# Two fused layers in fp32: one row sum in fp32, a first period in another order, and a scale and shift put off by way of memory

## The chip, the cores and the metric

The kernel runs on one core of a Trainium2 chip. A core has TensorE (PE, matmuls; PEld is its weight load), VectorE (DVE), ScalarE (ACT), GpSimd (POOL) and SyncE (SP), which mainly issues DMAs. The engines have separate in-order instruction streams and meet through semaphores. The metric is the device time of one execution in microseconds (us), as the median of several; smaller is better. The profile is of one execution, with time counted from its first instruction.

## What is computed

Four images of 64 by 64 positions with 256 channels pass through two layers, all in float32.

```python
# layer A: attention over the 4096 positions of an image
f, g, v = xt @ Wf + bf, xt @ Wg + bg, xt @ Wh + bh          # 32, 32, 128 channels
beta = softmax(einsum('bqd,bkd->bqk', g, f), axis=-1)
x = x + (einsum('bqk,bkd->bqd', beta, v) @ Wo + bo).reshape(b, h, w, c)
# layer B: triangle attention, 8 heads of 32, then a feed-forward
scores = einsum('bilhd,bljhd->biljh', q, k) / sqrt(d_k)
att = softmax(scores, axis=2)
out = einsum('biljh,bilhd,bljhd->bijhd', att, v1, v2)
h = layer_norm(x_in + out.reshape(B, N, N, E) @ Wo, ln_agg_g, ln_agg_b)
mlp = relu(h @ W1 + b1) @ W2 + b2
return layer_norm(mlp + h, ln_out_g, ln_out_b)               # scale ln_out_g, shift ln_out_b
```

## The kernel before

`run` goes through the images b = 0 to 3 in turn: layer A by `layer0`, then layer B by `first_layer1` (b = 0) or `next_layer1` (b = 1 to 3). The feed-forward of an image (class `Tokens`, instance `rest`) is not done in its own layer B but is woven into the layer B of the next image, 16 tiles of 256 positions; that of the last image ends in `alone`. So the feed-forward of image 0 runs in the layer B of image 1, that of image 1 in the layer B of image 2, and those of image 2 and of part of image 3 in the layer B of image 3. The schedule is by hand (`tc.manual_schedule`): each engine runs its instructions in the order in which the program issues them, and only the semaphores are put in by the framework.

**Layer A.** `layer0` walks 64 groups g, eight for each of eight blocks of 512 queries (`qb, k = divmod(g, 8)`). `score` makes four 128x512 score tiles in fp32r (L544), ScalarE takes their exponentials e (L556), and `values` multiplies them with v in fp32 (L571), while VectorE adds e up in esum (L578). At k = 7 the row sums of the block are made: VectorE folds esum to 512 columns (L581), writes a rounded fp32r part (L583), the sum once more in fp32 (L584), and the rest of it, sum minus part, again as fp32r (L585). `norm` multiplies both parts with a matrix of ones (L592), which adds them over the partitions in one PSUM tile den; the reciprocal (L594) and a product with o (L596) follow. The list `parts` spreads the projections of the block before over the groups k, each with its stores on SP. After the last block its parts stand apart: `norm(last)`, for an older image's feed-forward two `heads`, a projection, `output(last)` (y, L617), and then, mixed, the first scores of layer B, the rest of the projections and the first feed-forward tile. GpSimd has no work within the groups of layer A for b > 0.

**Layer B.** 32 steps (4 head pairs times 8 groups of rows), two of them in a period. A step has eight products of 128x2048 elements: att times v2 (`product`, L989), to be multiplied on TensorE with a sparse matrix of v1 (`accumulate`, L999) into the PSUM tiles acc. For b > 0 GpSimd makes three of the eight in even steps and two in odd ones (`npool`: the last ones, m = 5, 6, 7 or 6, 7), from a copy of att in SBUF; VectorE makes the others, with att in PSUM. VectorE's buffers R are three, GpSimd's buffers Rp two; a buffer is free when TensorE has accumulated it. ScalarE copies a finished acc out (`take`, L1009).

The order is the list `ORDER`: each word is a piece of work, and `/n` says by how many periods late it works (word `A05/1` in period p is the accumulation of product 5 of step 2(p-1)). Words: R product, A accumulate, T take, S sums, W weights, V the sparse matrix, t and c the turned attention weights; sp and e0, e1 a tile of scores and its exponentials for later periods, sf, f0, f1 the same for the first one alone; h0, h1 the heads of a feed-forward tile (L1058, L1063), sa its statistics, fa its first normalisation, ht, hT, hU the turned copies, m0, m1 and r0, r1 the hidden layer, z0, z1 its output (L1211), so the output's statistics (L1089, L1093), rr and pp the roots and their polishing (on GpSimd, L1119 to L1130), fo the last normalisation, and fi the last scale and shift. fi calls `finish`: two operations of 128x512 on GpSimd (L1225, L1226) and a store on SP (L1227). The tile z that it works on has tag s4, which has two buffers; the turned copies hT2 of the feed-forward use the same tag.

In steps 24 to 32 of a layer B the next image's inputs of layer A are fetched (`ahead.fetch` on SP, `ahead.spread` by DMAs that GpSimd issues, L260 and L266), for b < 3.

Of the kernel before, what the change touches and what calls it, by code (L numbers as in the profile page):

```python
# [10 lines left out]
F32 = mybir.dt.float32  # L11
# [4 lines left out]
ALU = mybir.AluOpType  # L16
AX = mybir.AxisListType

P = 128
C = 256  # L20
# [9 lines left out]
NP = T // 256  # L30
# [12 lines left out]
ORDER = """  # L43
    r0/1 A10/2 A11/2 m1/1 R14/2 R05/1 S1/1 R15/2 T10/2 sp/1 A14/2 A16/2 r1/1 e0/1 e1/1 A15/2 A05/1 T11/2 R04/1
    A04/1 z0/1 W1/1 R03/1 V1/1 fi/2 S0 z1/1 t1/1 so/1 R06/1 R00/1 c1/1 sa A03/1 R07/1 R02/1 A06/1 A02/1 A00/1
    rr/1 pp/1 W0 R01/1 A07/1 A01/1 fo/1 fa T01/1 R12/1 t0 T00/1 sf/1 R17/1 h1/-1 R13/1 f0/1 h0/-1 ht f1/1 R16/1
    hU A13/1 hT A12/1 A17/1 R11/1 c0 R10/1 m0 V0
""".split()

# [17 lines left out]
def attention_then_triangle_kernel(  # L67
# [422 lines left out]
    def layer0(b, F, safe, rest, ahead):  # L490
# [70 lines left out]
        def values(g, ahead):  # L561
            qb, k = divmod(g, 8)
            tt, n = divmod(k, 4)
            if k == 0:
                o_ps[qb] = pc("o")
                esum[qb] = work.tile([P, 4, QB], F32, tag="Rp", name="esum")
            es = e.pop(g)
            for r in range(4):
                if ahead:
                    score(g + 1, r)  # L570
                nc.tensor.matmul(  # L571
                    o_ps[qb], F.v[tt][:, r * 4 + n, :], es[:, r, :],
                    start=(k == 0 and r == 0), stop=(k == 7 and r == 3),
                )
            if k == 0:
                nc.vector.tensor_copy(esum[qb], es)
            else:
                nc.vector.tensor_tensor(esum[qb], esum[qb], es, ALU.add)  # L578
            if k == 7:
                halves = esum[qb]  # L580
                nc.vector.tensor_tensor(halves[:, 0:2], halves[:, 0:2], halves[:, 2:4], ALU.add)  # L581
                part = parts_of[qb] = work.tile([P, 2, QB], PART, tag="hid", name="part", bufs=1)
                nc.vector.tensor_tensor(part[:, 0], halves[:, 0], halves[:, 1], ALU.add)  # L583
                nc.vector.tensor_tensor(halves[:, 2], halves[:, 0], halves[:, 1], ALU.add)  # L584
                nc.vector.tensor_tensor(part[:, 1], halves[:, 2], part[:, 0].bitcast(F32), ALU.subtract)  # L585


        def norm(qb):
            den, part = pb("den") if qb < last else pa("den")[:, 0, :], esum.pop(qb)[:, 2, :]
            two = parts_of.pop(qb)  # L590
            for h in range(2):
                nc.tensor.matmul(den, ones_f, two[:, h], start=(h == 0), stop=(h == 1))  # L592
            rec = work.tile([P, QB], F32, tag="es", name="rec0")
            nc.vector.reciprocal(rec, den)  # L594
            oT[qb] = work.tile([P, QB], F32, tag="hT", name="oT")
            nc.vector.tensor_tensor(oT[qb], o_ps.pop(qb), rec, ALU.mult)  # L596
            ends[qb] = ((den, ALU.min), (part, ALU.max))
# [125 lines left out]
        for g in range(8 * NQB):  # L723
            qb, k = divmod(g, 8)
            if b == 0 and not safe:
                for load in later[3 * g : 3 * g + 3]:
                    load()
                if g == 6:
                    fold_bias()
                if g == 20:  # L730
                    add_b2()
            if safe and k == 0 and qb + 1 < NQB:
                mx, todo = pieces(qb + 1)
                for qc, t in todo:
                    max_piece(qc, t, mx)
                row[qb + 1] = max_row(mx)
            values(g, g + 1 < 8 * NQB)

            if qb > 0 and not (qb == last and k >= 6 + late):
                for part in parts[k]:  # L740
                    part(qb - 1)
            if late and g % 2 == 0 and 0 <= g // 2 - 2 < ahead.n:
                ahead.bring(g // 2 - 2)
            if late and g % 2 == 1 and 0 <= g // 2 - 3 < ahead.n:
                ahead.turn(g // 2 - 3)
            if qb == last and k == 3:
                L.fetch_v1(0)
                L.fetch_v1(1)
            if qb == last and k == 5:
                if b > 0:  # L750
                    rest.load(NP * (b - 1))
                L.fetch_qk(0, True)
# [273 lines left out]
    class Tokens:  # L1026
        def __init__(self):
            self.ios = []
            self.A, self.htp = {}, {}
            self.h, self.hT, self.hT2, self.hid, self.z, self.zp, self.hps = {}, {}, {}, {}, {}, {}, {}  # L1030
            self.mv = self.rs = None

        def load(self, tt, far=False):
            b, t = divmod(tt, NP)
# [394 lines left out]
    def next_layer1(b, L, rest, ahead, F):  # L1429
# [32 lines left out]
        def of_piece(word, q):  # L1462
# [9 lines left out]
            elif word == "sa" and first:  # L1472
                moments(q - 1)
                rest.stats(rest.hps[t0 + q], 0)
            elif word == "so" and second:
                moments(q)
                z = rest.z[t0 + q] = work.tile([P, 2, C], F32, tag="s4", name="z")
                rest.sums_of(rest.zp[t0 + q], z, rest.mv, 2)
            elif word == "rr" and second:
                moments(q)  # L1480
                rest.roots(0 if q + 1 < n1 else 2, 4)
                rs[q] = rest.rs
            elif word == "pp" and second:
                moments(q)
                rest.rs = rs.pop(q)
                rest.polish(0 if q + 1 < n1 else 2, 4, nc.gpsimd, back=back_t)
                rn[q] = rest.rn
            elif word == "fa" and first:
                rest.rn = rn[q - 1]
                rest.affine_a(tt)  # L1490
            elif word == "fo" and second:
                rest.rn = rn[q]
                rest.affine_o(tt)
            elif word == "ht" and first:
                rest.turn(tt)
            elif word == "hT" and first:
                rest.normed(tt)
            elif word == "hU" and first:
                rest.carried(tt)
            elif word in ("m0", "m1") and first:  # L1500
                n = int(word[1])
                mps[q][n] = [rest.hidden(tt, fc) for fc in (2 * n, 2 * n + 1)]
            elif word in ("r0", "r1") and first:
                n = int(word[1])
                for fc, mp in zip((2 * n, 2 * n + 1), mps[q][n]):
                    rest.rectify(tt, fc, mp)
            elif word in ("z0", "z1") and second:
                n = int(word[1])
                rest.outputs(tt, n, new=tt not in rest.zp)
                mps.setdefault(q, {})["z", n] = True  # L1510
            elif word == "fi" and second:
                rest.finish(tt)

        def spread(step):
            if F is not None:
# [4 lines left out]
        for period in range(NP + 4):  # L1520
            for word, late in words_of(ORDER):
                i = period - late
                if word[0] in "RATSWVtc":
                    step_word(word[0], 2 * i + int(word[1]), int(word[-1]))
                elif word in ("sp", "sf"):
                    if (i == 0) == (word == "sf"):
# [77 lines left out]
```

## Time and profile before

| what | value |
|---|---|
| runs shown | 3672.42 us median of 3 (3669.09 to 3676.33) |
| the profiled execution | 3669.47 us, its span 3667.7 us |
| TensorE busy | 3543.8 us (97%) |
| VectorE busy | 2725.4 us (74%) |
| ScalarE busy | 1935.7 us (53%) |
| GpSimd busy | 1760.0 us (48%) |
| L989 on GpSimd | 328 products, 4574 ns each |
| L989 on VectorE | 696 products, 2274 ns each |
| L1225 and L1226 on GpSimd | 48 each, 1288 and 1289 ns |
| L578 on VectorE | 224 adds, 2289 ns each |
| the chain that ended last | PE 67%, POOL 10%, issue 5%, DVE 4%, ACT 2% |

A busy time is the sum over an engine's instructions; since the engines work side by side, a share says little of what bounds a stage. The chain of waits is followed back from the last instruction to whatever released it. "idle before" names the engine whose work ended a wait. An fp32 matmul shows as two records, an fp32r matmul as one.

### The profile page before, as it was taken

To read this page: it belongs to the slowest core of one execution; us is meant where nothing else is said; L and a number is where in the kernel's file an instruction comes from. 1 tells how busy PE (TensorE), PEld (TensorE's weight loads), DVE (VectorE), ACT (ScalarE), POOL (GpSimd) and SP (SyncE) were. 2 spreads that over 40 slices of the span, in tenths; PEclk is the share of its full clock that TensorE was granted. 3 is DMA by queue.
4 is the path that set the end of the run, shared out by engine and by line. 5 is a ranking of instruction groups with operands and counts; after the bars stand their busy time and mean duration, and the time that the engine had idled before them with its cause. 6 is when DMAs were issued, how large, how long until landed. Compare 5 with 4: busy or idle time off the path is not lost.

```text
span 3667.7 us, 58399 instructions
## 1 busy us (share of the span) xinstructions
PE 3543.8 (97%) x22410; PEld 1909.1 (52%) x22410; DVE 2725.4 (74%) x2334; ACT 1935.7 (53%) x4209; POOL 1760.0 (48%) x918
## 2 busy tenths in 40 slices
PE   9999899889999999998999999999899999999998
PEld 6555444434555555553455555554455555555477
DVE  4777599997555489999555549999755556999976
ACT  3444455544444466765444446776444436777654
POOL 5000199994000089999000029999600005999920
PEclk9999999999999999999999999999999999999999
DMA  9544565464111444325311154333511125441221
GB/s 174 139 134 119 135 156 140 113 148 112 57 53 52 107 101 98 91 55 93 77 49 55 49 140 93 86 82 62 117 43 52 49 82 132 96 93 49 68 68 53
DMA packets 478769, 336.59 MB, mean 92 GB/s; under 512 B 301648, under 2 KB 432464, under 8 KB 469648
## 3 DMA queue, kind: packets, MB, share of 16 engines
q1 hardware_dynamic: 429440, 305.80, 31.5%
q0 software_dynamic: 36160, 19.94, 5.1%
q10 hardware_dynamic: 12880, 7.01, 0.7%
q8 instruction: 179, 2.93, 0.3%
q14 instruction: 110, 0.90, 0.1%
HBM read 188.95 MB, written 143.65 MB: 91 GB/s over the span
## 4 chain that ended last, share of the span: by engine, by line
PE 67%; POOL 10%; issue 5%; DVE 4%; ACT 2%; DMA 0%; ACTq 0%; POOLq 0%; DVEq 0%
PE o L571 18%; PE acc L999 16%; POOL Rp L989 8%; PE proj L632 6%; PE zp L1211 5%; PE mp L1191 5%; PE s L544 5%; PE hp L1058 3%; PE sp L887 2%; DVE R L989 2%; PE v1p L664 2%; PE y L617 1%; PE att L941 1%; PE hp L1063 1%; PE htp L1158 1%
## 5 line engine op out<-in xcount | busy, mean ns | idle before, releaser
L989 POOL TENSOR_TENSOR Rp<-attP,v 128x2048 f32<-128x2048 f32 x328 | 1490.6, 4574 | 403.6 <-ACT attP L949 368.9
L989 DVE TENSOR_TENSOR R<-att,v 128x2048 f32<-128x2048 f32 x696 | 1548.4, 2274 | 81.3 <-PE acc L999 62.9
L571 PE MATMUL o<-e,v 128*128 128x512 f32 x2048 | 1043.6, 592 | 0.0
L578 DVE TENSOR_TENSOR esum<-esum,e 128x2048 f32<-128x2048 f32 x224 | 512.7, 2289 | 518.0 <-ACT e L556 515.1
L556 ACT ACTIVATE e<-s 128x1024 f32<-128x1024 f32 x512 | 523.3, 1023 | 580.8 <-PE s L544 482.0
L544 PE MATMUL s<-gT,fT 128*128 128x512 f32 x1024 | 785.3, 769 | 8.1 <-ACT e L556 5.1
L999 PE MATMUL acc<-R,wsel 128*32 128x512 f32 x5568 | 704.4, 601 | 31.2 <-DVE R L989 20.0
L1119 POOL TENSOR_SCALAR nt<-mv 128x4 f32<-128x4 f32 (+1 forms) x51 | 9.8, 192 | 1204.1 <-DVE mv L1075 1200.0
L571 PEld LDWEIGHTS o<-e,v 128*128 128x128 f32 x2048 | 388.6, 190 | 275.9 <-issue 233.7
L999 PE MATMUL acc<-Rp,wsel 128*32 128x512 f32 x2624 | 345.4, 598 | 32.9 <-POOL Rp L989 32.3
L1009 ACT COPY ao<-acc 128x1024 f32<-128x1024 f32 x256 | 254.3, 1021 | 183.5 <-PE acc L999 146.4
L999 PEld LDWEIGHTS acc<-R,wsel 128*32 128x32 f32 x5568 | 152.6, 109 | 377.4 <-issue 279.7
L544 PEld LDWEIGHTS s<-gT,fT 128*128 128x128 f32 x1024 | 194.0, 190 | 243.5 <-issue 230.5
L924 ACT ACTIVATE es<-S,rd 128x64 f32<-128x64 f32 x1024 | 257.9, 336 | 16.7 <-DVE rd L916 13.9
L1191 PE MATMUL mp<-hT,w 128*128 128x256 f32 x1024 | 249.5, 389 | 0.7 <-ACT hT L1163 0.7
L1211 PE MATMUL zp<-w,hid 128*128 128x256 f32 x1024 | 245.0, 385 | 0.8 <-ACT hid L1200 0.8
L1191 PEld LDWEIGHTS mp<-hT,w 128*128 128x128 f32 x1024 | 186.7, 190 | 101.3 <-ACT attP L949 36.0
L1211 PEld LDWEIGHTS zp<-w,hid 128*128 128x128 f32 x1024 | 185.6, 190 | 62.4 <-issue 31.9
L594 DVE RECIPROCAL rec<-den 128x512 f32<-128x512 f32 x32 | 107.4, 3357 | 125.2 <-PE den L592 125.2
L999 PEld LDWEIGHTS acc<-Rp,wsel 128*32 128x32 f32 x2624 | 80.7, 110 | 220.1 <-issue 124.9
L1200 ACT ACTIVATE hid<-mp,b_sb 128x256 f32<-128x256 f32 x256 | 105.3, 470 | 117.7 <-PE mp L1191 117.7
L897 ACT ACTIVATE S<-sp 128x512 f32<-128x512 f32 x128 | 129.8, 1116 | 64.5 <-PE sp L887 64.5
(177 smaller groups left out, 3563.0 us busy)
## 6 DMA issues: line engine op xcount, KB each, us to landing
v<-v2d SPq DMA_DIRECT2D x44, 512.0 KB
v1c<-v1d SPq DMA_DIRECT2D x128, 128.0 KB
aT<-ao SPq DMA_DIRECT2D x1024, 16.0 KB
A<-aT SPq DMA_DIRECT2D x256, 64.0 KB
out_dram<-z SPq DMA_DIRECT2D x63, 256.0 KB
y<-yT SPq DMA_DIRECT2D x56, 256.0 KB
q<-st SPq DMA_DIRECT2D x56, 256.0 KB
k<-st SPq DMA_DIRECT2D x52, 256.0 KB
```

The lines of the kernel that those rows point to most:

```text
L544: nc.tensor.matmul(s_ps[r // 2][:, r % 2, :], fT[tt][:, ts(r * 4 + n, P)], gT[qb // 4][:, ts(qb % 4, QB)], start=True, stop=not safe,)
L556: nc.scalar.activation(e[g][:, 2 * j : 2 * j + 2, :], s_ps[j], AF.Exp)
L571: nc.tensor.matmul(o_ps[qb], F.v[tt][:, r * 4 + n, :], es[:, r, :], start=(k == 0 and r == 0), stop=(k == 7 and r == 3),)
L578: nc.vector.tensor_tensor(esum[qb], esum[qb], es, ALU.add)
L632: nc.tensor.matmul(ps, w[:, cc, rows], y(qb, cc), start=(cc == 0), stop=(cc == 1))
L897: nc.scalar.activation(self.S[pair][:, :, l0 : l0 + 8].rearrange("p i l -> p l i"), sp[:, lh], AF.Copy if self.safe else AF.Exp,)
L924: nc.scalar.mul(e[:, i, :], rows[:, i, :], rec[:, i : i + 1])
L989: eng.tensor_tensor(R, src.unsqueeze(1).to_broadcast([P, D, N]), v2[h], ALU.mult)
L999: nc.tensor.matmul(acc[32 * c : 32 * c + 32, n % 2, :], w[:, n, c, 16 * h : 16 * h + 32], R[:, ts(c, 8), :].rearrange("p d j -> p (d j)"), ...
L1009: nc.scalar.copy(self.ao[step][:, ts(np, 2)].rearrange("p k d j -> p k (d j)"), self.acc[step][np])
L1191: nc.tensor.matmul(self.mp[:, fc % 2, :], w1_sb[:, cc, ts(fc, P)], self.hT[tt][:, cc, :], start=(cc == 0), stop=(cc == 1),)
L1211: nc.tensor.matmul(zp[:, n, :], self.hid[tt][:, fc, ts(n, P)], w2_sb[:, fc, :], start=(fc == 0), stop=(fc == 3 and tt not in self.hT2),)
```

## The change

It has three parts.

1. For the last block of layer A (`qb == last`) VectorE no longer writes the two fp32r parts: after the fold it makes one fp32 sum, and `norm` multiplies it with the ones in one fp32 matmul.
2. In `ORDER`, h1 stands ahead of sf, and h0 ahead of f0. sf, f0 and f1 do something in the first period only, so only there does the order change. For step 0 the accumulations of products 5 and 4 change places.
3. For b = 1 and 2, fi calls `put_off` in place of `finish`: the normalised tile is stored unscaled to DRAM. In the layer A of the next image, `recall` loads a tile back at every third group, and `finish` scales, shifts and stores it two groups later. The layer B of image 3 keeps `finish`.

```diff
 ORDER = """
-    rr/1 pp/1 W0 R01/1 A07/1 A01/1 fo/1 fa T01/1 R12/1 t0 T00/1 sf/1 R17/1 h1/-1 R13/1 f0/1 h0/-1 ht f1/1 R16/1
+    rr/1 pp/1 W0 R01/1 A07/1 A01/1 fo/1 fa T01/1 R12/1 t0 T00/1 R17/1 h1/-1 sf/1 R13/1 h0/-1 f0/1 ht f1/1 R16/1
...
             if k == 7:
                 halves = esum[qb]
                 nc.vector.tensor_tensor(halves[:, 0:2], halves[:, 0:2], halves[:, 2:4], ALU.add)
+                if qb == last:
+                    nc.vector.tensor_tensor(halves[:, 2], halves[:, 0], halves[:, 1], ALU.add)
+                    return
...
         def norm(qb):
             den, part = pb("den") if qb < last else pa("den")[:, 0, :], esum.pop(qb)[:, 2, :]
-            two = parts_of.pop(qb)
-            for h in range(2):
-                nc.tensor.matmul(den, ones_f, two[:, h], start=(h == 0), stop=(h == 1))
+            if qb < last:
+                two = parts_of.pop(qb)
+                for h in range(2):
+                    nc.tensor.matmul(den, ones_f, two[:, h], start=(h == 0), stop=(h == 1))
+            else:
+                nc.tensor.matmul(den, ones_f.bitcast(F32), part, start=True, stop=True)
...
+            if b > 1 and g % 3 == 0 and g < 3 * NP:
+                rest.recall(NP * (b - 2) + g // 3)
+            if b > 1 and g % 3 == 2 and g < 3 * NP:
+                rest.finish(NP * (b - 2) + g // 3)
...
+            self.raw = {}
+        def put_off(self, tt):
+            b, t = divmod(tt, NP)
+            if t == 0:
+                self.raw[b] = dram.tile([NP, P, 2, C], F32, tag="raw", name="raw")
+            nc.sync.dma_start(out=self.raw[b][t], in_=self.z.pop(tt))
+
+        def recall(self, tt):
+            b, t = divmod(tt, NP)
+            self.z[tt] = work.tile([P, 2, C], F32, tag="s4", name="z")
+            nc.sync.dma_start(out=self.z[tt], in_=self.raw[b][t])
...
             elif word == "fi" and second:
-                rest.finish(tt)
+                (rest.finish if own else rest.put_off)(tt)
...
-                if word[0] in "RATSWVtc":
+                if i == 0 and word in ("A05", "A04"):
+                    for m in (4, 5) if word == "A04" else ():
+                        step_word("A", 0, m)
+                elif word[0] in "RATSWVtc":
                     step_word(word[0], 2 * i + int(word[1]), int(word[-1]))
```

## The prediction

> **What bounds the kernel now.** I read the page's slices first, then windows by stage, the waits of each engine in a stage, and the timeline where a stage starts or ends. Times are us from the span's start; A and B name the two layers (spatial attention, triangle attention).
>
> ```profile
> PE   9999899889999999998999999999899999999998
> POOL 5000199994000089999000029999600005999920
> ```
>
> Each digit is a fortieth of the span. TensorE is full nearly everywhere. GpSimd is empty in each image's layer A and full in layer B, where it takes 5 of every 16 products (L989) and the scale and shift L1225, L1226. Windows over images 1, 2, 3 (bounds; length; then busy PE, PEld, DVE, ACT, POOL; clock; DMA):
>
> ```profile
> 1760.00:2130.00 370.00, 370.00 (x1036) 195.77 (x1035) 198.85 (x131) 154.58 (x174) 0.00 (x0) 1.00 0.17 53
> 1400.00:1605.00 205.00, 205.00 (x1869) 110.69 (x1871) 198.70 (x141) 143.99 (x393) 197.03 (x102) 1.00 0.34 79
> 1605.00:1747.00 142.00, 129.51 (x953) 59.31 (x945) 131.18 (x87) 82.46 (x240) 138.09 (x83) 0.98 0.42 80
> 2487.00:2629.00 142.00, 128.44 (x964) 59.48 (x956) 131.47 (x87) 82.62 (x240) 138.09 (x84) 0.99 0.43 79
> 3372.00:3510.00 138.00, 134.44 (x960) 67.80 (x952) 133.47 (x103) 87.00 (x252) 128.31 (x69) 1.00 0.21 54
> ```
>
> In layer A (first row) and in the body of layer B (second), TensorE is busy every microsecond: a saving on another engine is worth nothing there. A period of the body is 27.76 us. In the tail (last 5 periods of layer B, rows 3 and 4) the scores are all made, TensorE falls behind, and GpSimd is full (138.1 of 142). Image 3's tail (row 5) has no next image to fetch for. What GpSimd does in one tail period of image 1:
>
> ```profile
> 1677.40 9.06 POOL L989 TENSOR_TENSOR Rp<-attP,v 128x2048 f32<-128x2048 f32 x2
> 1686.40 1.36 POOL L260 DMA_DIRECT2D gT<-ahgf  x2
> 1687.78 4.59 POOL L989 TENSOR_TENSOR Rp<-attP,v 128x2048 f32<-128x2048 f32 x1
> 1692.32 1.30 POOL L1225 TENSOR_TENSOR z<-z,log_bc 128x512 f32<-128x512 f32 x1
> 1693.69 1.28 POOL L1226 TENSOR_TENSOR z<-z,lob_bc 128x512 f32<-128x512 f32 x1
> 1694.93 4.55 POOL L989 TENSOR_TENSOR Rp<-attP,v 128x2048 f32<-128x2048 f32 x1
> ```
>
> No gap: each entry starts as the one before ends. 1692.32 to 1694.93 is 2.61 us for scale and shift. The waits in 1626 to 1747 (total, times, longest) show who pays:
>
> ```profile
> PE acc L999 <- POOL Rp L989: 8.7, 5, 2.7
> DVE R L989 <- PE acc L999: 7.9, 6, 2.7
> ```
>
> **What the Trainium skill says.** "FP8 and Floating Point Precision", TensorE Precision Notes: true fp32 takes 4 passes through the array. The trace agrees: an fp32r 128x512 matmul (L544) is one record with 0.23 us to the next, an fp32 one (L571) two records 0.43 apart, so 0.86. "GPSIMD Engine Reference", Key points: GpSimd shares its SBUF interfaces with VectorE, with contention against VectorE instructions of two SBUF inputs. No stretch of this trace shows it: L989 reads one operand from PSUM, and GpSimd sleeps while L578 (both in SBUF) runs. "DMA: Bandwidth & Descriptors", Anatomy of one DMA: a semaphore wait happens on the issuing sequencer, so a waiting DMA blocks SP's queue. "TensorE: Matmul & The Clock Gate", Part 1: idle windows of about 3.4 us halve the clock. Seen here: in 2195.8 to 2199.7 the granted clock was 0.57.
>
> **Part 1, row sums of the last block (4 images).** The end of layer A, image 1:
>
> ```profile
> 1256.39 0.69 DVE L583 TENSOR_TENSOR part<-esum 128x512 fp32r<-128x512 f32 x1
> 1257.00 0.68 DVE L584 TENSOR_TENSOR esum<-esum 128x512 f32<-128x512 f32 x1
> 1257.72 0.69 DVE L585 TENSOR_TENSOR part<-esum,part 128x512 fp32r<-128x512 f32 x1
> 1258.47 0.50 PE L592 MATMUL den<-part,ones_f 128*128 128x512 f32 x1 [0.77 <-DVE part L585]
> 1259.00 3.36 DVE L594 RECIPROCAL rec<-den 128x512 f32<-128x512 f32 x1 [0.59 <-PE den L592]
> ```
>
> Two of the three adds go, and two fp32r matmuls become one fp32. Before, the reciprocal starts 2.61 after 1256.39. After: one add to 1257.07, about 0.1 to start the matmul, 0.43 for its first record, and 0.53 from the last record to the reciprocal (1258.47 to 1259.00): 1258.2, so 0.8 sooner. By y (L617), whose first reader starts 1.17 after it, it is 0.63. I take 0.75. TensorE's cover while VectorE takes the reciprocal, 4 us of heads and a projection, moves along by the same, and the 0.29 us wait before y stays. 4 x 0.75 = 3.0; bounds 2.5 to 3.4.
>
> **Part 2, the first period's words (images 1 to 3).**
>
> ```profile
> 1299.18 1.07 PE L999 MATMUL acc<-Rp,wsel 128*32 128x512 f32 x8 [1.32 <-POOL Rp L989]
> 1313.09 2.08 PE L887 MATMUL sp<-q,k 32*64 32x64 f32 x64 [1.58 <-ACT ao L1009]
> 1315.10 1.13 PE L1058 MATMUL hp<-wo,A 128*128 128x256 f32 x4
> ```
>
> A04 now precedes A05: its 0.86 us falls in the 1.32 wait for GpSimd's first product. But the next point, 1313.09, hangs on GpSimd: three products from 1294.60 to 1308.2, then the polish, then ScalarE's two affine passes and its first copy of acc. None of these moves for A04, so this swap gives 0 by itself. The other swap gives more: h1 (0.86 + 0.22 = 1.08 us) moves ahead of the scores sf. It needs its PSUM buffer, free when the second affine pass ends at 1312.13, so it runs about 1312.17 to 1313.25 and scores follow there, not at 1313.09. The stretch to the end of h0 ends 0.92 sooner. ScalarE's f0, f1 move 0.16 later and still end before ht's copies are due. Its tokens were asked of SP at 1297.67, 14 us ahead. 3 x 0.92 = 2.8; bounds 0 (if h1 waits for its load) to 3.2.
>
> **Part 3, scale and shift put off (feed-forwards of images 0 and 1, so the layers B of images 1 and 2).** It takes 2.61 us from GpSimd in each of 16 periods. In the body that only lengthens the wait GpSimd already has before its next product (0.48 at 1441.32, for TensorE to release a buffer): gain 0. In the tail, four of these lie ahead of the last product, which ends at 1744.84. The first (1632.51) lets the product behind it start when its buffer is free, 6.7 before the next statistics at 1640.33, as in the body: 1633.6 for 1635.12, 1.5 us. The other three give 7.83. GpSimd alone would end 9.3 sooner. VectorE is next: its 7.9 us of waits are all that can go, of which I leave 0.4 standing: 7.5. Image 3's tail speaks for it: with scale and shift but no fetches (2.67 a period, nearly the same price) its periods are 27.2 for 29.9, and VectorE waits 0.2 us in all. Image 2's waits are 8.1. Two tails: 15.0; bounds 2 x 3.5 and 2 x 9.
>
> What it adds: the store L1227 becomes a store of the raw tile, same size and place in SP's queue; its value (L1135) was ready a period before. In layer A of images 2 and 3: 16 loads of 256 KB, 16 stores, 32 GpSimd operations, one tile in three groups (19 us), hidden by TensorE, DMA at 0.17 and an idle GpSimd. On SP, behind a load that waits stand the q, k, v stores of layer A; but a load's buffer was freed four groups before, and a store's operation ran a group before. Contention: 2 x 1.29 us beside L578; VectorE is busy 199 of 370, but at each block's border it is late (ScalarE waits up to 3.0 for L578), so some may show. Below nothing it can't go. I take 0.5 in all; bounds 0 and 83 (32 x 2.58, each in full on the path).
>
> **Clock.** In image 3 the granted clock was 0.66 in 3021 to 3026, behind part 1's pause (1.00 at image 1's), and y starts 5.36 us after the reciprocal for 4.14. With one pause for two I take 1.0 as saved; bounds -3 and 4, since such windows fall as they may.
>
> Sum: 3.0 + 2.8 + 15.0 + 1.0 - 0.5 = 21.3. The profiled execution took 3669.5 (span 3667.7), the median is 3672.4, 2.9 above: 3648.2 for its like, 3651 for the median.
>
> **Rivals.**
> - Tails gain half (TensorE's fixed order and three R buffers keep VectorE waiting): 2 x 3.5 for 15, so 13.3 in all: 3659. For: its waits name TensorE, not GpSimd. Against: image 3.
> - Tails gain nothing, as another chain (ScalarE's copies of acc, 2.3 us of waits) ends there: 6.3 in all: 3666. Against: only two such waits.
> - Slower: GpSimd's deferred operations hold up L578 at its shared SBUF interface, VectorE releases e late, ScalarE's exponentials and TensorE's values follow. At 1.29 us on the path for each of 32 tiles, 41 us: 3651 + 41 = 3692. It decides from (21.8 + 7.3) / 32 = 0.9 us a tile. For: TensorE has no slack in layer A. Against: VectorE is idle for 46% and only 7 borders an image are tight.
>
> **How the numbers follow.** Forecast 0.70 (own range 3644 to 3657), half tails 0.12, none 0.06, slower 0.08, more than forecast 0.04. A measurement of this kernel tells 0.2% (7.3 us) from no change. Faster: 0.70 + 0.12 + 0.04, less a little of the second's edge: 0.85; same 0.07; slower 0.08. The range 3642 to 3665 takes in the half tails.
>
> **What would show it.** Tail periods of images 1 and 2 near 27.2, with VectorE's waits there under 2 us; GpSimd waiting about 3 us a period in the body, whose period stays 27.76; the reciprocal 0.75 sooner after L581; h1 right behind the affine pass; layer A of images 2 and 3 still full on TensorE with L578 at 2289 ns. The forecast fails if L578 grows and TensorE gets gaps in layer A, if SP's stores bunch behind loads, or if the tails keep 29.9.

## The result and the profile after

The changed kernel takes 3651.59 us (median of 4 runs, 3650.9 to 3654.27); the kernel before took 3674.38 beside it (4 runs, 3669.09 to 3676.82). The ratio is 0.9941, with a 95% interval of 0.9924 to 0.9958. In a later set of runs the two stood at 3653.27 (5 runs) and 3674.94 (9 runs), ratio 0.9939 (0.9925 to 0.9952).

The profiled execution took 3654.27 us with a span of 3652.5, so that its span is only 15.2 shorter than that of before. The stages tell why (us; each stage from its first to its last matmul, B's from the first `acc`):

| stage | before | after |
|---|---|---|
| image 0, both layers | 822.4 | 827.9 |
| image 1, both layers | 880.6 | 872.1 |
| image 2, both layers | 882.5 | 872.4 |
| image 3, both layers | 878.1 | 875.3 |
| images 1 to 3 together | 2641.1 | 2619.8 |

Images 1 to 3 are 21.3 shorter. Image 0 is 5.4 longer in this execution: its layer B takes 421.93 for 415.96, though it issues the same instructions in both kernels. The granted clock was at half for 22.2 us of it, for 8.2 before. (A time in which TensorE's granted clock is 0.5 is called a half-clock stretch below.) Over the fourteen profiled executions of this study that stage took 415.1 to 422.7, and it went with the clock: 415.1 to 418.4 in the six with 4.8 to 11.9 us at half clock, 419.2 to 422.7 in the eight with 16.1 to 22.9.

The two rows of the page's slices that were shown before:

```profile
PE   9999899988999999999999999999999999999998
POOL 5000199994000068889311028889722106999910
```

Of GpSimd's four 9s in the layers B of images 1 and 2 three have become 8s, and its four zeros in the next layers A now read 3110 and 2210. Line numbers are each kernel's own: L999 and L1009 of the changed kernel are L989 and L999 of the kernel before. The windows by stage of the changed kernel (bounds; length; busy PE, PEld, DVE, ACT, POOL; clock; DMA), in the order of before: layer A of image 2, body of image 1, tails of images 1, 2 and 3:

```profile
1765.00:2130.00 365.00, 365.00 (x1023) 193.23 (x1022) 204.50 (x129) 152.27 (x172) 59.35 (x31) 1.00 0.23 72
1405.00:1605.00 200.00, 200.00 (x1807) 107.48 (x1809) 193.75 (x136) 140.98 (x389) 174.35 (x87) 1.00 0.33 79
1610.00:1744.40 134.40, 125.79 (x932) 58.62 (x921) 130.14 (x87) 82.36 (x239) 126.25 (x75) 1.00 0.46 85
2482.00:2616.70 134.70, 127.44 (x941) 59.06 (x933) 130.43 (x87) 82.38 (x239) 126.47 (x75) 0.99 0.42 85
3357.00:3494.00 137.00, 133.38 (x955) 67.08 (x948) 132.54 (x100) 86.35 (x251) 128.17 (x69) 1.00 0.22 54
```

Layer A keeps TensorE full with 59 us of GpSimd's work in it. In the body GpSimd is busy 174 of 200 instead of 197 of 205, and a period is still 27.76. The tails are shorter: the starts of the statistics L1142 (L1119 before) lie 27.23, 27.28, 27.33 and 25.97 apart in image 1, for 28.62, 29.87, 29.86 and 28.55. That is 9.1 us less; but from the last of these starts to the end of the layer it is 15.04 for 12.88, so 6.9 is left for the layer. One tail period on GpSimd's timeline now holds products and fetches alone:

```profile
1677.93 9.08 POOL L999 TENSOR_TENSOR Rp<-attP,v 128x2048 f32<-128x2048 f32 x2
1686.95 1.36 POOL L260 DMA_DIRECT2D gT<-ahgf  x2
1688.33 9.12 POOL L999 TENSOR_TENSOR Rp<-attP,v 128x2048 f32<-128x2048 f32 x2
```

The waits in that tail (1627 to 1744.4; total, times, longest) have changed sides:

```profile
PE acc L1009 <- DVE R L999: 5.4, 6, 2.6
...
DVE R L999 <- PE acc L1009: 1.7, 1, 1.7
...
PE acc L1009 <- POOL Rp L999: 1.1, 2, 0.9
```

The kernel before had, beside the two lines that the prediction shows:

```profile
PE acc L999 <- DVE R L989: 0.4, 1, 0.4
```

TensorE waited 8.7 us for GpSimd's products and now waits 1.1; VectorE's 7.9 are 1.7; what TensorE now waits for is VectorE (5.4 for 0.4). The end of layer A of image 1, from the timeline, first the fold of the kernel before, then the changed kernel:

```profile
1255.13 1.23 DVE L581 TENSOR_TENSOR esum<-esum 128x1024 f32<-128x1024 f32 x1
```

```profile
1261.25 1.23 DVE L581 TENSOR_TENSOR esum<-esum 128x1024 f32<-128x1024 f32 x1
1262.51 0.69 DVE L583 TENSOR_TENSOR esum<-esum 128x512 f32<-128x512 f32 x1
1263.35 1.10 PE L598 MATMUL den<-esum,ones_f 128*128 128x512 f32 x2 [1.23 <-DVE esum L583]
...
1264.48 3.36 DVE L600 RECIPROCAL rec<-den 128x512 f32<-128x512 f32 x1 [1.28 <-PE den L598]
```

The reciprocal starts 3.23 after the fold L581 starts; before it was 3.87 (1255.13 to 1259.00). TensorE has one pause there, 1.23, and not two. In the first period the heads go into what was one pause:

```profile
1315.59 0.66 PE L951 MATMUL att<-ident,es 128*128 128x128 f32 x4
...
1316.80 1.13 PE L1081 MATMUL hp<-wo,A 128*128 128x256 f32 x4 [0.55 <-ACT z L1158]
1317.76 0.38 PE L1086 MATMUL hp<-ident,yc 128*128 128x128 f32 x2
1318.61 1.64 PE L897 MATMUL sp<-q,k 32*64 32x64 f32 x49 [0.46 <-ACT ao L1019]
```

h1 (L1081, L1086) stands behind the affine pass L1158, and the scores follow. The period is 30.18 for 31.19. One thing went against the list of signs: L578 is not at 2289 ns. Its mean over the whole kernel is 2344; in layers A of images 2 and 3, where the put-off work runs, it is 2405 and 2391, and the longest takes 3381. GpSimd's scale and shift take 1.60 and 2.32 us there, for 1.29 each.

### The profile page after: what moved, and what is told of

Read it like the earlier page. It is cut to its first block, busy times and chain, and to the rows that moved or that the text cites. A ratio compares the mean times of both kernels' runs of the same rounds, so it can differ in the third digit from the quotient of the medians.

```text
span 3652.5 us, 58549 instructions
## 1 busy us (share of the span) xinstructions
PE 3544.0 (97%) x22410; PEld 1909.6 (52%) x22410; DVE 2739.5 (75%) x2326; ACT 1934.8 (53%) x4209; POOL 1805.7 (49%) x918
## 4 chain that ended last, share of the span: by engine, by line
PE 68%; POOL 5%; DVE 4%; issue 3%; ACT 2%; DMA 1%; SPq 0%; ACTq 0%; DVEq 0%; POOLq 0%
PE o L571 18%; PE acc L1009 15%; PE proj L638 6%; PE mp L1214 6%; PE zp L1234 5%; PE s L544 5%; POOL Rp L999 4%; DVE R L999 3%; PE sp L897 3%; PE hp L1081 3%; PE v1p L670 2%; PE y L623 1%; PE att L951 1%; PE htp L1181 1%; PE hp L1086 1%
## 5 line engine op out<-in xcount | busy, mean ns | idle before, releaser
L999 POOL TENSOR_TENSOR Rp<-attP,v 128x2048 f32<-128x2048 f32 x328 | 1491.1, 4576 | 463.3 <-ACT attP L959 367.8
L999 DVE TENSOR_TENSOR R<-att,v 128x2048 f32<-128x2048 f32 x696 | 1547.7, 2274 | 67.7 <-PE acc L1009 49.4
L578 DVE TENSOR_TENSOR esum<-esum,e 128x2048 f32<-128x2048 f32 x224 | 525.0, 2344 | 508.9 <-ACT e L556 505.6
L1009 PE MATMUL acc<-R,wsel 128*32 128x512 f32 x5568 | 705.7, 602 | 37.2 <-DVE R L999 29.4
L1009 PE MATMUL acc<-Rp,wsel 128*32 128x512 f32 x2624 | 344.3, 596 | 11.1 <-POOL Rp L999 10.4
L1009 PEld LDWEIGHTS acc<-R,wsel 128*32 128x32 f32 x5568 | 152.1, 109 | 384.5 <-issue 277.9
L1142 POOL TENSOR_SCALAR nt<-mv 128x4 f32<-128x4 f32 (+1 forms) x51 | 9.8, 192 | 627.2 <-DVE mv L1098 623.1
L1248 POOL TENSOR_TENSOR z<-z,log_bc 128x512 f32<-128x512 f32 x48 | 71.8, 1496 | 452.2 <-DMA z<-raw 434.5
L1009 PEld LDWEIGHTS acc<-Rp,wsel 128*32 128x32 f32 x2624 | 81.5, 110 | 197.8 <-issue 139.0
```

The costliest lines, as they stand in the source:

```text
L999: eng.tensor_tensor(R, src.unsqueeze(1).to_broadcast([P, D, N]), v2[h], ALU.mult)
L1009: nc.tensor.matmul(acc[32 * c : 32 * c + 32, n % 2, :], w[:, n, c, 16 * h : 16 * h + 32], R[:, ts(c, 8), :].rearrange("p d j -> p (d j)"), ...
```

## The experiments

Theory: the three parts add up, each in its own place, and layer A hides what was put off. The rivals were that one part carries another's gain, that the body gains too, that GpSimd's work beside VectorE costs layer A time, and, once the first traces were in, that half-clock stretches fall anywhere.

### Each part alone

Each is the kernel before with one part of the diff put in.

**Row sums alone** (L581 to L598 of the change).

```diff
+                if qb == last:
+                    nc.vector.tensor_tensor(halves[:, 2], halves[:, 0], halves[:, 1], ALU.add)
+                    return
...
```

> The kernel before with part 1 alone. My theory: the reciprocal of each last block starts 0.6 to 0.8 us sooner after the fold (3.87 us before), the whole gains 2 to 3 us, and the stretch from that reciprocal to layer B's first accumulation stays 40.2 us in images 1 to 3. Rival (the fp32 matmul's two records and their drain eat what the two adds gave): under 0.3 us a block, nothing in all. In the changed kernel image 0 showed 0.39 and the others 0.64; if image 0 shows 0.39 again, it is its own, not the run's.

The one execution took 3666.31, the kernel before beside it 3675.77 (9 runs). The trace shows the reciprocal 3.23 behind the fold in images 1 to 3 (3.87 before) and 3.48 in image 0 (3.88); no other stage of images 1 to 3 moved but by half-clock stretches. That is 3 x 0.64 + 0.40 = 2.3. The rest of the distance in time is not in these places: this execution had a granted clock of 0.994, the nine of the kernel before 0.991 to 0.993, and a single execution can't price the part.

**A04 and A05 exchanged alone.**

```diff
-                if word[0] in "RATSWVtc":
+                if i == 0 and word in ("A05", "A04"):
+                    for m in (4, 5) if word == "A04" else ():
+                        step_word("A", 0, m)
+                elif word[0] in "RATSWVtc":
```

> The kernel before with the exchange of A04 and A05 in the first period alone. My theory: layer B's first accumulation starts 1.3 us sooner (38.8 us after the reciprocal, 40.2 before), but the first scores of the period still wait for ScalarE's copy of acc and start at the same time after the reciprocal, 54.1 us, so the gain is 0. Rival: TensorE is what bounds the first period, and the scores start 0.86 us sooner.

The one execution took 3679.32. The first `acc` of an image starts some 1.4 us sooner, and image 3's layer B, without a half-clock stretch in either kernel, takes 445.33 from there for 443.83: what is moved ahead is waited out later. The first periods are 31.19 and 31.20 as before (image 1's 32.88 has a half-clock stretch in it). TensorE's timeline in image 1 shows where it goes:

```profile
1319.45 0.66 PE L941 MATMUL att<-ident,es 128*128 128x128 f32 x4
1322.47 2.08 PE L887 MATMUL sp<-q,k 32*64 32x64 f32 x64 [2.36 <-ACT ao L1009]
```

The pause ahead of the scores has grown from 1.58 to 2.36 and they start when ScalarE lets them. The exchange by itself gains 0.

**h1 and h0 ahead of sf and f0 alone.**

```diff
-... T00/1 sf/1 R17/1 h1/-1 R13/1 f0/1 h0/-1 ht f1/1 R16/1
+... T00/1 R17/1 h1/-1 sf/1 R13/1 h0/-1 f0/1 ht f1/1 R16/1
```

> The kernel before with the heads ahead of the scores in the first period alone. My theory: the heads fill the 1.58 us wait before the scores, and the accumulations behind them start 0.9 us sooner after the reciprocal in each of images 1 to 3: 2.8 us in all. Rival (the heads wait for their load or their PSUM buffer): 0 or later.

The one execution took 3665.49. The first periods are 30.12, 30.12 and 30.11 for 31.19: 1.07 us for each of three images. TensorE in image 1:

```profile
1311.96 1.06 PE L1071 MATMUL hp<-wo,A 128*128 128x256 f32 x4
1312.85 0.38 PE L1076 MATMUL hp<-ident,yc 128*128 128x128 f32 x2
1313.70 2.08 PE L887 MATMUL sp<-q,k 32*64 32x64 f32 x64 [0.47 <-ACT ao L1009]
```

The scores start 54.1 us after the reciprocal in image 3, as they did before, so h1 costs nothing where it now stands. Part 2's gain is h1's place in the pause, not the other exchange.

**Scale and shift put off alone.**

```diff
-                rest.finish(tt)
+                (rest.finish if own else rest.put_off)(tt)
...
+            if b > 1 and g % 3 == 0 and g < 3 * NP:
+                rest.recall(NP * (b - 2) + g // 3)
+            if b > 1 and g % 3 == 2 and g < 3 * NP:
+                rest.finish(NP * (b - 2) + g // 3)
```

> The kernel before with part 3 alone. My theory: tail periods of images 1 and 2 go from 28.6, 29.9, 29.9, 28.6 us to 27.3, 27.3, 27.3, 26.0, the body's stay 27.76, layer A stays 389.0, and the whole gains 13 to 15 us (3659 for 3674). Rival (a good part of what the changed kernel gained is not the tails but the first periods and the clock's half-speed windows there): under 10 us.

It took 3661.61 (6 runs) beside 3675.77, ratio 0.9966 (0.9953 to 0.9978): 14.2 us. The layer B of image 1 is 440.80 from its first `acc` for 447.67, so 6.87; the four periods before the end are 27.22, 27.32, 27.32 and 25.95. Image 2 is the same within 0.05 once a half-clock stretch in its first period is taken out of both. Layers A of images 2 and 3 take 389.13 and 389.14 (389.02, 389.04). The whole of part 3 is in the tails: 13.7. The clock is no rival for it: image 2's tail has one half-clock stretch before and one here, and gains the same 6.9 as image 1's, where two stretches went.

### Which tiles have to be put off

These two are the changed kernel with only the first eleven tiles of an image put off, or only the last five; `recall` and the later `finish` are limited to the same tiles.

```diff
...
-                (rest.finish if own else rest.put_off)(tt)
+                (rest.put_off if not own and q < 11 else rest.finish)(tt)
```

> The changed kernel, but of the 16 tiles of an image only the first 11, whose scale and shift fall in layer B's body, are put off; the other five are scaled and shifted in place, in the tail. My theory: the body is bound by TensorE, so these 11 are worth nothing: tail periods of images 1 and 2 are back at 28.6, 29.9, 29.9, 28.6 us, and the time is that of parts 1 and 2 alone, about 3667 for 3674. Rival (GpSimd enters the tail ahead because it was relieved in the body): a part of the 13.7 us stays, 3 us or more.

3664.32 (6 runs) beside 3674.68 (10 runs), ratio 0.997 (0.9958 to 0.9983), for an expected 3667. The tails are those of the kernel before (28.63, 29.89, 29.90, 28.56), and TensorE and VectorE wait for the same things there (1632 to 1749):

```profile
PE acc L1009 <- POOL Rp L999: 9.3, 7, 2.7
```
```profile
DVE R L999 <- PE acc L1009: 8.1, 6, 2.2
```

The body's period is 27.76 with and without scale and shift. GpSimd then only waits longer: in 1405 to 1605 of the changed kernel its products wait 15.5 us for TensorE to release a buffer, 3.1 at a time; before, over 1400 to 1605, 3.4 in all. The 2.7 us under the expected time are not traced to a stage; they are not in the tails.

```diff
...
-                (rest.finish if own else rest.put_off)(tt)
+                (rest.put_off if not own and q > 10 else rest.finish)(tt)
```

> The changed kernel, but only the last five tiles of an image, whose scale and shift fall in layer B's tail, are put off. My theory: all of the gain is here: tail periods 27.3, 27.3, 27.3, 26.0 us and the time of the changed kernel, 3651 to 3652, with 22 of 32 tiles fewer on the way through memory. Rival (the relief in the body counts too): 3 us or more slower than the changed kernel.

3649.56 (4 runs), ratio 0.9934 (0.9917 to 0.995). Tail periods 27.29, 27.32, 27.36 and 25.99, layers A 389.02 and 389.02. Five tiles give all that sixteen give, with two thirds of the added traffic gone. Its interval overlaps that of the changed kernel, so it isn't shown to be faster.

### What GpSimd's work in layer A costs

The changed kernel with the scale and shift of each put-off tile done three times (its output is scaled and shifted three times).

```diff
-            eng.tensor_tensor(z, z, log_bc.unsqueeze(1).to_broadcast([P, 2, C]), ALU.mult)
-            eng.tensor_tensor(z, z, lob_bc.unsqueeze(1).to_broadcast([P, 2, C]), ALU.add)
+            for again in range(3 if b < 2 else 1):
+                eng.tensor_tensor(z, z, log_bc.unsqueeze(1).to_broadcast([P, 2, C]), ALU.mult)
+                eng.tensor_tensor(z, z, lob_bc.unsqueeze(1).to_broadcast([P, 2, C]), ALU.add)
```

> The changed kernel, with the scale and the shift of the 32 tiles that are put off done three times on GpSimd in layer A (with this scale and shift the values stay as they are). GpSimd then works some 9 us in each 19. In the changed kernel its operations took 1.50 us for 1.29, and L578 2.34 for 2.29, yet layer A stayed at 389.0 us. My theory: L578 goes to 2.4 or 2.5 us in the mean, VectorE still has the room, and layer A gains under 2 us an image. Rival (the one on the slower side: the shared interface holds up L578 where VectorE is late): layer A grows by 5 us or more in images 2 and 3 and stays at 389 in image 1.

3659.5 (5 runs), ratio 0.9959 (0.9945 to 0.9974): 6 to 8 us above the changed kernel's two medians. Layers A of images 2 and 3 take 393.38 and 391.75 for 389.12 and 389.06, so 7.0 of it is there. The theory (under 2 us an image) failed; the slower rival (5 or more) came nearer with 4.3 and 2.7. Its GpSimd and VectorE early in layer A of image 2:

```profile
1759.64 2.29 DVE L578 TENSOR_TENSOR esum<-esum,e 128x2048 f32<-128x2048 f32 x1 [2.06 <-ACT e L556]
...
1763.14 1.28 POOL L1250 TENSOR_TENSOR z<-z,lob_bc 128x512 f32<-128x512 f32 x1
1763.99 2.59 DVE L578 TENSOR_TENSOR esum<-esum,e 128x2048 f32<-128x2048 f32 x1 [2.06 <-ACT e L556]
1764.51 3.21 POOL L1249 TENSOR_TENSOR z<-z,log_bc 128x512 f32<-128x512 f32 x1
1767.79 1.28 POOL L1250 TENSOR_TENSOR z<-z,lob_bc 128x512 f32<-128x512 f32 x1
1768.33 2.88 DVE L578 TENSOR_TENSOR esum<-esum,e 128x2048 f32<-128x2048 f32 x1 [1.76 <-ACT e L556]
```

The shift takes 1.28 when VectorE stands still, the scale 3.21 beside L578; L578 takes 2.29 alone and 2.59 or 2.88. The Trainium skill's "GPSIMD Engine Reference", Key points, says that the two share their SBUF interfaces and contend where a VectorE instruction has two SBUF inputs; this trace agrees, with 3.21 for 1.28. The ends show how. In the traces of this kernel and of the changed one, 74 scales or shifts start while an L578 runs, and each ends 1.12 to 1.15 us behind it; 47 times L578 starts 0.05 us or more behind a scale or shift that has 0.2 us or more to run, and each time it ends 2.14 to 2.15 behind. That is nearly the whole time that each takes alone, so the one that starts second waits for the first. Between groups VectorE has about 2 us of idle time, and nothing follows. It shows at the first border between two blocks of an image, where VectorE's adds are on the path:

```profile
1783.79 1.60 POOL L1250 TENSOR_TENSOR z<-z,lob_bc 128x512 f32<-128x512 f32 x1
1784.18 1.76 DVE L587 TENSOR_TENSOR esum<-esum 128x512 f32<-128x512 f32 x1
...
1785.47 1.59 POOL L1249 TENSOR_TENSOR z<-z,log_bc 128x512 f32<-128x512 f32 x1
1785.97 1.63 DVE L588 TENSOR_TENSOR part<-esum,part 128x512 fp32r<-128x512 f32 x1
...
1787.66 0.69 PE L596 MATMUL den<-part,ones_f 128*128 128x512 f32 x1 [1.95 <-DVE part L588]
```

Two adds of 0.68 and 0.69 take 1.76 and 1.63, TensorE pauses 1.95, and a half-clock stretch follows. The window of the same kernel:

```profile
1787.80:1791.40 3.60, 3.60 (x7) 1.92 (x8) 3.60 (x2) 0.45 (x1) 0.95 (x1) 0.53 0.47 129
```

At the second border between blocks the trace is 3.8 us later than the changed kernel's in image 2 (1.95 of it is this pause, most of the rest follows at half clock) and 2.7 in image 3, which has no such stretch. So the slower rival's mechanism is there, and it costs without the clock too. With one scale and shift a tile it met no border on the path; with three it did.

### GpSimd's fetches

The changed kernel with the spreads of g and of f's low half, for images 2 and 3, issued on SP's queue instead of GpSimd's.

```diff
-        nc.gpsimd.dma_start(
+        (nc.gpsimd if queue is None else queue).dma_start(
...
-                    spread_g(F, step - 24, d, half)
+                    spread_g(F, step - 24, d, half, nc.sync if b > 1 else None)
...
-                    spread_f(F, r, d, 0)
+                    spread_f(F, r, d, 0, nc.sync if b > 1 else None)
```

> The changed kernel, with the twelve DMAs of the next image's g and f that GpSimd issues in the tail issued by SP instead (images 1 and 2). It takes 2.7 us more from GpSimd in a tail period. My theory: GpSimd with 27.3 us a period is the bound that is left, VectorE with 26.9 the next; tail periods of images 1 and 2 go to 26.9 and the whole gains 1 to 2 us. Rival one: VectorE is the bound already, and nothing changes. Rival two: the DMAs wait in SP's queue ahead of layer B's stores, and the tail gets longer.

3650.24 (4 runs), ratio 0.9941 (0.9924 to 0.9958), so no gain. Image 1's first tail periods fall to 25.83 and 26.46, VectorE waits only 0.3 us for TensorE in that tail, and the layer B is 439.72 for 441.16. So in the changed kernel GpSimd still set the first tail periods, though TensorE's waits there name VectorE. Image 2's tail starts alike, but its last period has a half-clock stretch, and its layer B is 441.43 for 441.26. Then layers A of images 2 and 3 take 390.10 and 390.31: ScalarE's third exponential comes 1.0 and 1.2 us later, in image 2 behind a wait of 4.78 us that the profile puts down to a transfer issued on SP (3.79 in the changed kernel, put down to TensorE). What image 1's tail gained came back as a late start.

### The half clock

In images 1 to 3 the first traces had half-clock stretches at the end of layer A only in the kernels with the old row sums, and in the first period of layer B only in those with the old order. The end of layer A, where the last block's row sums are made, is called the border here. To see whether that was chance, the changed kernel was run again beside itself with part 1, or the heads' part of part 2, undone.

> The changed kernel once more, as the measure for the three runs beside it. Theory (a pause in front of a border makes a half-clock window): no window within 60 us behind the last block's reciprocal at any of the three borders, reciprocal 3.23 after the last fold, tail periods 27.2 to 27.4. Time 3651.5 within 3, ratio 0.994. Rival (windows fall at random): some border has a window as often as in the kernel before, about 0.8 a border.

3653.27 (5 runs); no half-clock stretch at any border or first period; tail periods 27.25, 27.32, 27.33, 25.96.

```diff
-                if qb == last:
-                    nc.vector.tensor_tensor(halves[:, 2], halves[:, 0], halves[:, 1], ALU.add)
-                    return
...
```

> The changed kernel with part 1 undone (three adds and two fp32r matmuls again). Theory (part 1 is worth its 0.64 a border, 0.39 in image 0, and also removes half-clock windows at the border): the reciprocal is 3.87 after the last fold, and at least one of the three borders shows a half-clock window within 8 us of the reciprocal, each worth 1.1 us: 2.3 + about 1.9, so some 4 us slower than the changed kernel, 3655.7. Rival (windows fall at random, part 1 is worth its instructions alone): 2.3 slower and no more windows at the borders than the changed kernel has.

In place it did as the theory said. The reciprocal is 3.87 behind the fold in image 3, and 4.15 in images 1 and 2, where a half-clock stretch lies. TensorE and the window there in image 1:

```profile
1260.20 0.47 PE L592 MATMUL den<-part,ones_f 128*128 128x512 f32 x1 [1.23 <-DVE part L583]
...
1261.44 0.78 PE L592 MATMUL den<-part,ones_f 128*128 128x512 f32 x1 [0.77 <-DVE part L585]
1262.02 1.91 PE L1075 MATMUL hp<-wo,A 128*128 128x256 f32 x4
```
```profile
1261.35:1264.90 3.55, 3.46 (x9) 2.79 (x10) 2.67 (x2) 0.00 (x0) 0.00 (x0) 0.52 1.00 218
```

Two pauses, 1.23 and 0.77, then clock 0.52: four matmuls of L1075 take 1.91, while L1081 took 1.03 there in the changed kernel. From fold to first `acc` the three images take 43.77, 43.65 and 42.67, the changed kernel 42.02 to 42.03: 1.7 + 1.6 + 0.6, with image 0's 0.4 some 4.4. The time is 3653.86 (5 runs), though, only 0.6 above the changed kernel and not the expected 4. In its profile image 0's layer B is 4.2 shorter than in the changed kernel's second profile, with 11.4 us at half clock for 22.9. Whether that is chance isn't settled, so the 4.4 is shown in place and not in the time.

```diff
-... T00/1 R17/1 h1/-1 sf/1 R13/1 h0/-1 f0/1 ht f1/1 R16/1
+... T00/1 sf/1 R17/1 h1/-1 R13/1 f0/1 h0/-1 ht f1/1 R16/1
```

> The changed kernel with h1 and h0 behind sf and f0 again; A04 stays ahead of A05. Theory: first period 31.19 again for 30.1, 1.06 us for each of three images, and a half-clock window of 1.7 us at one border in four: 3.2 + 1.3, so 4.5 slower than the changed kernel, 3656. Rival (A04's place gives part of the gain): first period under 31, less than 3 us slower.

3660.12 (5 runs), 6.9 above the changed kernel, for an expected 4.5. The layers B are 1.9, 1.7 and 3.2 longer, 6.8 together, and all three first periods have a half-clock stretch (32.08, 31.91 and 33.41 us; the last has one of double length). TensorE in image 1, and the window:

```profile
1314.29 0.66 PE L951 MATMUL att<-ident,es 128*128 128x128 f32 x4
1317.32 2.09 PE L897 MATMUL sp<-q,k 32*64 32x64 f32 x64 [2.37 <-ACT ao L1019]
1319.33 1.94 PE L1081 MATMUL hp<-wo,A 128*128 128x256 f32 x4
```
```profile
1317.40:1321.00 3.60, 3.60 (x68) 3.20 (x69) 1.53 (x1) 2.33 (x3) 3.60 (x2) 0.53 0.10 20
```

Over all profiled executions, three images each:

| TensorE's pauses | kernels | half-clock stretch behind |
|---|---|---|
| border, 1.23 and 0.77 | five with the old row sums | 9 of 15 |
| border, 1.23 | nine with the new row sums | 0 of 27 |
| first period, 2.36 | swap alone; heads undone | 4 of 6 |
| first period, 1.58 | before; sums alone; put-off alone | 2 of 9 |
| first period, about 0.5 (twice in the changed kernel) | nine with h1 ahead | 0 of 27 |

Chance alone would hardly leave the two classes with the shorter pauses at 0 of 27 each; the pauses decide whether a stretch can come. The exchange of A04 and A05 makes the pause longer where h1 doesn't fill it, so it is safe only beside the other exchange.

### A version of both

Only the last five tiles put off, and g's spreads alone on SP.

```diff
+            if b > 1 and g % 3 == 0 and g < 3 * NP and g // 3 > 10:
...
+                    spread_g(F, step - 24, d, half, nc.sync if b > 1 else None)
```

> Only the last five tiles of an image are put off, and in the tails of images 1 and 2 the fetches of the g half go from GpSimd's queue to SP's; those of f stay on GpSimd. Theory (GpSimd's work still sets the first tail periods, SP has room): tail periods 25.8 and 26.5 first, then 26.9 and 26.0, 1.8 us less a tail; layer A of the next image as long as in the changed kernel (389.0), for its start was late by 1.2 us only where f's fetches stood in SP's queue; 3 us or so under the same kernel with g's fetches on GpSimd: about 3647, ratio 0.993. Rival (what SP takes over comes back as a late start of layer A, or TensorE sets the tail): layer A 390 or tail periods 27.2, time as the changed kernel, 3650 to 3652.

3647.96 (5 runs, 3645.12 to 3651.01), ratio 0.9924 (0.991 to 0.9937), against 3653.27 and 0.9939 (0.9925 to 0.9952) for the changed kernel on the same chip. Layers A are 389.13 and 389.12 as hoped. The tail gains 1.5 us in image 2 and nothing in image 1, where 25.90 and 26.44 are followed by 28.29 and 27.11 with two half-clock stretches among them. It has the lowest median of the last four, near the expected 3647, but that isn't the expected 1.8 a tail: the intervals overlap, the trace shows only 1.5 of the 5.3, and the same kernel with g's fetches on GpSimd took 3649.56. It is faster than the kernel before, not shown to be faster than the changed one.

## Why the prediction was right

The mechanism of each part is the one that was forecast, and the large terms are near. That the time came out within a microsecond is in part luck: parts 1 and 3 were put too high, the clock too low, and the drop was 22.8 from 3674.4 where 21.3 from 3672.4 had been forecast.

- **Part 1**, 3.0 predicted, 2.3 in place: 0.64 a border and not 0.75, and 0.4 in image 0. The forecast's own sum gives 1258.13 and so 0.87, which it wrote as 0.8. The matmul started 0.15 behind the add and not 0.1, and the reciprocal 1.13 behind the matmul's start for 0.43 + 0.53. The figure by y, 0.63 a border, was the right one.
- **Part 2**, 2.8 predicted, 3.1 in place (1.0, 1.0 and 1.1 in images 1, 2 and 3 of the profiled pair, clock apart). The exchange of A04 and A05 gives 0, as worked out, though what it does to the pause was left out; h1 in ScalarE's shadow gives all, 1.07 alone for 0.92, for the scores behind it don't start 0.16 later, as forecast, but at their old time.
- **Part 3**, 15.0 predicted, 13.7 in place. Tail periods came as image 3's had promised, 9.1 us less in all, near the 9.3 worked out for GpSimd alone; the layer's end gained 6.9. The cap of 7.9 by VectorE's waits held; 1.7 of them were left in image 1, not 0.4, and the run with the fetches on SP shows GpSimd still behind that rest. The body gave nothing, shown by the run without the tail's tiles.
- **Layer A**, 0.5 predicted, 0.1 or less in place. But the expectation that L578 stays at 2289 ns failed: in these layers it went to 2405 and 2391, and GpSimd's shift to 2.32 us from 1.29. The contention exists; the idle time of VectorE, named as its cover, covered it. SP's queue waited in front of the put-off stores four times, 28.0 us in all in layer A of image 2, with nothing behind it on TensorE, as that layer's 389.12 us show. (The 2.34 and 1.50 us that the run with the work tripled was set against are means over all images, and so too low.)
- **Clock**, 1.0 predicted, 2.8 in the profiled pair: a border stretch in image 3 (1.1) and a first-period stretch in image 2 (1.7), both gone. As an estimate from the table, 9 of 15 x 3 images x 1.1 + 2 of 9 x 3 x 1.7 = 3.1. This is the most mis-sized term: the prediction let such stretches fall as they may, and the pauses that parts 1 and 2 take away are what sets them. It had read the stretch at 2196 as an idle window of 3.4 us; TensorE's pause ahead of it was 1.58.

In images 1 to 3 of the profiled pair the terms make 1.9 + 3.1 + 13.7 + 2.8 - 0.1 = 21.4, and the stages show 21.3. The rivals with half of the tails' gain or none of it fell with the periods of 27.3. The slower rival had its mechanism right and its place wrong: its point of decision, 0.9 us a tile on the path, was never near, for the path was touched only at the first border between blocks, and only with the work tripled.

What stays open is image 0's layer B, which spans 7.6 us over the profiled executions though its instructions and their order are the same in every kernel. It follows its time at half clock; what sets that isn't shown. The eight long ones all come from kernels with the exchange of A04 and A05 (eight of ten, none of the four without), so that it is chance isn't shown either. In the profiled pair it takes 6.0 us from the gain, which is most of why the spans differ by 15.2 only. For the medians there are no stages, but a clock: 28 executions of the kernel before had 0.991 to 0.995 and took 3677.5 us in the mean at 0.991, 3672.8 at 0.993 and 3665.9 in the one at 0.995; nine of the changed kernel had 0.994 to 0.996. A swing of this size is also why the price of part 1 could not be read from the time.

## What to carry to other kernels

When TensorE's pause is shortened or filled, count the half-clock stretch behind it too: here filling a pause of 2.37 us with 1.1 us of heads was worth 6.9 us over three images, more than twice the 3.2 us that the heads gained by themselves. Moving work off a full engine paid here only in the stage where TensorE's waits named that engine, so only the tiles of that stage need be put off. The list of waits isn't the whole of it, though: after the change it named VectorE, while GpSimd's fetches still set the first tail periods. Work given to GpSimd beside two-input VectorE operations should be kept away from the points where VectorE's result is waited for.

## What the runs showed of the hardware

- Half-clock stretches are 3.41 us long, or two or once three times that; only the one that each execution ends in is cut off by the end. In one execution their starts lie whole multiples of 3.413 us apart over the whole span: those of the kernel before in images 1 and 2 at 487.00, 497.00, 631.01 and 737.01 times 3.4133 behind the first. The Trainium skill, "TensorE: Matmul & The Clock Gate", Part 1, describes such a free-running window of 3413 ns, so a pause meets it in one execution and misses it in another; the counts above agree. The same page (Why this matters for your kernels) puts the limit at gaps of about 3 us; here a gap of 1.58 was enough in 2 of 9, and 1.23 with 0.77 in 9 of 15. The grid settles which of the 15 borders: where a stretch came, the 3.41 us of the grid just before it held 1.78 to 2.00 us of TensorE's idle time; at the six without one no such window held more than 1.72, and with the new row sums none held more than 1.23. Elsewhere idle time alone doesn't decide: 2.02 brought no stretch in the changed kernel's first tail, and 0.82 was enough ahead of the stretch at 2196 in the kernel before, so what else counts isn't shown.
- A GpSimd 128x512 fp32 add or multiply takes 1.28 us alone and up to 3.4 beside a VectorE add of two SBUF operands, as the one that starts second waits for the other; VectorE's 128x2048 add goes from 2.29 to as much as 3.4, its 128x512 add from 0.69 to as much as 1.76. Beside VectorE's reciprocal, which reads PSUM, GpSimd's stay at 1.27 to 1.28.
- A half-clock stretch in a tail that GpSimd bounds costs nothing: in the kernel before, image 1's tail had two and image 2's one, with the same periods within 0.02 us.
